# Delta rule: how the keys reach their tokens, and where their sums of squares come from

## The chip, the core and the metric

The kernel runs on one core of a Trainium2 chip. The metric is the device time of one execution in microseconds; of several runs the median is taken. The core has TensorE (PE, with its weight loads PEld), VectorE (DVE), ScalarE (ACT), GpSimd (POOL) and SyncE (SP), which here only issues DMAs.

## The reference

One decoder layer on 4 sequences of 512 tokens with 512 features, all in float32: a gated delta rule (16 heads of 128), then cross attention, then causal attention, then a mixture of experts. The change lies in the delta rule:

```python
q = causal_conv(x @ Wq.T)   # 4 taps along the tokens, then silu; k and v alike
g = exp(-exp(A_log) * softplus(a + dt_bias));  beta = sigmoid(b)
q, k = l2norm(q), l2norm(k)                       # by head, over 128 features
def step(S, (q_t, k_t, v_t, g_t, beta_t)):
    error = v_t - g_t * (S.T @ k_t)
    S = g_t * S + outer(k_t, beta_t * error)
    return S, S.T @ q_t
```

The kernel computes the recurrence in chunks of 128 tokens: inside a chunk through the inverse of a triangular matrix made of the products of all keys, from chunk to chunk through the state S. For that each key is needed in two layouts: features on the partitions (`kT`, for products) and tokens on the partitions (`ktok`, for the update of the state, scaled to `kdec`), and the sum of squares of each token's key (`ss`).

## The kernel before

The delta rule takes the first 1790 us or so. Its unit is a pair of heads of one sequence; 4 sequences x 8 pairs make 32 rounds (`NP`, line 1107). A round m is a set of generators that are advanced in turns (`turns`, line 192): for each step of `stage3(m)` two steps of `stage1(m + 2)`, one of `stage2_values(m + 1)`, two of the inversions for pair m + 1, one of `output(m - 1)`, and around a change of sequence some of `prologue`. A `yield` in a generator ends its step. So the place of a line among the `yield`s of its generator sets what it stands beside.

- `conv` (line 592) projects 128 features (TensorE, L598, into a PSUM tile `pb`), scales on ScalarE (L606), adds three shifted copies on VectorE (L609) and applies silu (L612).
- `stage1` (line 617): the two keys by `conv`; then, in one step for each head, four TensorE transposes into a PSUM tile (L641), a copy to `ktok` (L643) and four squares with sums (L646) on ScalarE; then `ss` is clamped (L652, VectorE) and raised to the power -1/2 on GpSimd (L653), with the small products `ee`, `ke`, `nr` (L654 to L657); two scans on VectorE make the decays `em` (L662) from a row loaded by DMA (`rows(0)`, L625); in the next two steps `em` is scaled by `ee` on ScalarE (L458), the products of the keys are made (L671, a PSUM tile `pb`), and `at` = -products x `em` on VectorE (L674) goes to DRAM (L675). `load_blocks` (L740) brings its diagonal blocks to the inversion. Then come the queries and, in `decayed`, `kdec` from `ktok` (L458).
- `stage2_inverse` (line 743) eliminates in 31 steps on GpSimd (L751, L752; in the first two rounds on VectorE).
- `stage2_values` (line 788): values by `conv`, then `brought`: VectorE transposes 32x32 blocks into the SBUF tile `vt`, which has one buffer (L798), four DMAs write it to DRAM (`v_d`, L801), one reads it back with tokens on the partitions (`vn`, L806), and it is scaled (L809).
- `stage3` (line 852) joins the inverse from its blocks, then goes through the four chunks: `pk` and `r` (L918, L921), `pu` and its ScalarE copy `u` (L928, L930), the state (L938, L943 or L941), the outputs (L946, L948).
- `output` (line 973) projects to the 512 features (L992) and adds up in `xa` (L997).

GpSimd, VectorE and ScalarE run in the order in which this code issues (`manual_schedule`, line 1089). The orders of TensorE and of SP's DMA queue are left to the framework's planner. [...] The DMAs that these steps name are issued by SP.

Of the kernel before, what the change touches and what calls it, by code (L numbers as in the profile page):

```python
# [31 lines left out]
F32 = mybir.dt.float32  # L32
BF16 = mybir.dt.bfloat16
AF = mybir.ActivationFunctionType
ALU = mybir.AluOpType
AX = mybir.AxisListType
# [3 lines left out]
P = 128  # L40
B, S, D = 4, 512, 512
NT = B * S // P
TB = S // P
# [3 lines left out]
HG = 2  # L47
# [57 lines left out]
def decoder(ctx: ExitStack, tc: tile.TileContext, a: dict, out: bass.AP):  # L105
    nc = tc.nc
# [6 lines left out]
    ident = tab[:, C_ID, :]  # L113
# [68 lines left out]
    def run(*gs):  # L182
        for g in gs:
            for _ in g:
                pass
# [17 lines left out]
    dram = ctx.enter_context(tc.tile_pool(name="dram", bufs=1, space=DRAM))  # L203
# [174 lines left out]
    with ExitStack() as st:  # L378
# [10 lines left out]
        def lasting(m, name, of, shape):  # L389

            own = m % of == (B * NHG - 1) % of
            return live[own].tile(shape, F32, name=name, bufs=HG * (1 if own else of - 1))
# [59 lines left out]
        def chunks(t):  # L452
            return t.rearrange("p c j -> p (c j)")

        def scale(dst, src, by, p):

            for c in range(TB):
                nc.scalar.activation(dst[:, c, :], src[:, c, :], AF.Identity, scale=by[:, p * TB + c : p * TB + c + 1])  # L458

        def behind(engine):  # L460

# [122 lines left out]
        def load_weights(m, *what, by=nc.sync):  # L584

            for n in what:
                if m < B * NHG:
                    t = (s1 if n < 2 else s2).tile([P, KD, HG * P], F32, name=f"w{n}", bufs=1)
                    by.dma_start(t, a["a_w"][m % NHG][:, n])
                    weights[m, n] = t  # L590
# [23 lines left out]

        keys, pairs = {}, {}

        def stage1(m):

            b, hg = divmod(m, NHG)
            hh = slice(hg * HG, (hg + 1) * HG)  # L620
            wk, wq = weights.pop((m, 1)), weights.pop((m, 0))

            def rows(n):
                t = s1.tile([P, HG, S], F32, name=f"row{n}", bufs=1)
                nc.sync.dma_start(chunks(t), g_d[b, n, hg * HG * TB : (hg + 1) * HG * TB].rearrange("c t -> (c t)").partition_broadcast(P))  # L625
                return [t[:, p, :] for p in range(HG)]

            kT, kt = [], []
            ss = small.tile([P, HG * TB], F32, name="ss", bufs=2)
            for p in range(HG):  # L630
                t = lasting(m, "kT", 3, [P, S])
                yield from conv(b, hg, p, 1, wk, t)
                kT.append(t)
                yield
            xnT, beta, gam, ngam, gend, gall = seqs[b]
            gb = rows(0)
            load_weights(m + 1, 1)
            for p in range(HG):
                tp = p_b.tile([P, TB, P], F32, name="pb")
                for c in range(TB):  # L640
                    nc.tensor.transpose(tp[:, c, :], kT[p][:, c * P : (c + 1) * P], ident)  # L641
                t = s1.tile([P, TB, P], F32, name="ktok")
                nc.scalar.copy(t, tp)  # L643
                kt.append(t)
                for c in range(TB):
                    nc.scalar.activation(tp[:, c, :], tp[:, c, :], AF.Square, accum_out=ss[:, p * TB + c : p * TB + c + 1])  # L646
                yield

            rk, ee, ke = (small.tile([P, HG * TB], F32, name=n, bufs=2) for n in ("rk", "ee", "ke"))
            nr = small.tile([P, HG * TB], F32, name="nr", bufs=4)  # L650
            flat = lambda t: t[:, hh, :].rearrange("p h c -> p (h c)")
            nc.vector.tensor_scalar(ss, ss, 1e-24, None, ALU.max)  # L652
            nc.gpsimd.tensor_tensor(rk, ss, mhalf[:, 0 : HG * TB], ALU.pow)  # L653
            nc.gpsimd.tensor_tensor(ee, rk, rk, ALU.mult)  # L654
            nc.gpsimd.tensor_tensor(ee, ee, flat(beta), ALU.mult)
            nc.gpsimd.tensor_tensor(ke, ee, flat(gend), ALU.mult)
            nc.gpsimd.tensor_tensor(nr, ss, rk, ALU.mult)  # L657
            em = []
            for p in range(HG):

                e = s1.tile([P, TB, P], F32, name="em")
                nc.vector.tensor_tensor_scan(chunks(e), gb[p], id4, 0.0, ALU.mult, ALU.add)  # L662
                em.append(e)
                yield
            ats = []
            for p in range(HG):
                scale(em[p], em[p], ee, p)
                pk = p_b.tile([P, TB, P], F32, name="pb")
                for c in range(TB):
                    k_ = kT[p][:, c * P : (c + 1) * P]  # L670
                    nc.tensor.matmul(pk[:, c, :], k_, k_, start=True, stop=True)  # L671
                at = lasting(m, "at", 2, [P, TB, P])
                ats.append(at)
                nc.vector.scalar_tensor_tensor(at, pk, -1.0, em[p], ALU.mult, ALU.mult)  # L674
                nc.sync.dma_start(squares(at_d[m % SLOTS][p * TB : (p + 1) * TB]), at)  # L675
                yield
            load_blocks(m, ats)
            mb = rows(1)

            qh, qg, pt, sq, kd_ = [], [], [], [], []  # L680

            def product(p):
                pq = p_b.tile([P, TB, P], F32, name="pb")
                for c in range(TB):
                    cs = slice(c * P, (c + 1) * P)
                    nc.tensor.matmul(pq[:, c, :], kT[p][:, cs], qh[p][:, cs], start=True, stop=True)
                t = lasting(m, "pt", 3, [P, TB, P])
                nc.vector.tensor_tensor(t, pq, em[p], ALU.mult)
                pt.append(t)

            def decayed(p):
                t = lasting(m, "kdec", 2, [P, TB, P])
                scale(t, kt[p], ke, p)
                kd_.append(t)

            for p in range(HG):
                q = s1.tile([P, S], F32, name="qh")
                c = conv(b, hg, p, 0, wq, q)
                yield from itertools.islice(c, 2)
                if p:  # L700
                    product(0)
                yield from c
                qh.append(q)
                g = lasting(m, "qg", 3, [P, S])
                nc.gpsimd.tensor_tensor(g, q, mb[p], ALU.mult)  # L705
                qg.append(g)
                t = w2.tile([P, S], F32, name="cv", bufs=5)
                nc.scalar.activation(t, q, AF.Square)
                sq.append(t)
                yield  # L710
            load_weights(m + 1, 0)
            decayed(0)
            yield

            pss = p_b.tile([P, HG, P], F32, name="pb")
            for p in range(HG):
                for c in range(TB):
                    nc.tensor.matmul(pss[c * 32 : (c + 1) * 32, p, :], tab_a[:, C_ONE, 0:32], sq[p][:, c * P : (c + 1) * P], start=True, stop=True)
            sr = small.tile([P, HG, P], F32, name="sr", bufs=1)
            nc.scalar.copy(sr, pss)  # L720

            rq = small.tile([P, HG * TB], F32, name="rq", bufs=2)
            for p in range(HG):
                nc.sync.dma_start(rq[p * P // HG : (p + 1) * P // HG, :], sr[:, p, :].rearrange("(c x) (n k) -> x c n k", x=32, k=HG * TB)[0])
            yield
            product(1)
            yield
            decayed(1)
            yield
            keys[m] = (kT, kd_, qg, pt, nr, rq)  # L730
# [57 lines left out]
        def stage2_values(m):  # L788
# [5 lines left out]

            def brought(p, t):

                x = w2.tile([P, 4, TB, 32], F32, name="vt", bufs=1)
                nc.vector.transpose(x.rearrange("p b k i -> p k b i"), t.rearrange("p (k b j) -> p k b j", b=4, j=32))  # L798
                d = dram.tile([P, 4, P], F32, name="v_d", bufs=4)
                for q in range(4):  # L800
                    nc.sync.dma_start(d[:, q, :].rearrange("(b j) x -> j b x", b=4), x[q * 32 : (q + 1) * 32].rearrange("p b k i -> p b (k i)"))  # L801
                yield
                yield
                v = w2.tile([P, 4, TB, 32], F32, name="vn", bufs=4)
                v_.append(v.rearrange("p a k i -> p k a i"))
                nc.sync.dma_start(v.rearrange("p a k i -> p a (k i)"), d)  # L806
                yield
                yield
                nc.vector.tensor_tensor(v, v, nr[:, p * TB : (p + 1) * TB].unsqueeze(1).unsqueeze(3).to_broadcast([P, 4, TB, 32]), ALU.mult)  # L809
# [1115 lines left out]
```

## Time and profile before

| | us |
|---|---|
| median of 3 runs | 3317.46 (3315.84 to 3320.69) |
| the profiled execution, whole time | 3312.34 |
| its span | 3310.5 |
| TensorE busy in the span | 3134.8 (95%) |
| VectorE / ScalarE / GpSimd busy | 1877.9 / 1603.0 / 1487.7 |
| L641, transposes of the keys: TensorE busy | 40.8 (x256) |
| L643 and L646, copies, squares and sums: ScalarE busy | 37.7 (x64), 67.1 (x256), 49.7 (x256) |
| L662, scans: VectorE busy | 74.7 (x64) |
| L671, products of the keys: TensorE busy | 66.9 (x512) |
| L798, block transposes of the values: VectorE busy | 45.4 (x64) |

In a line of the timeline stand the start in us from the start of the span, the time it lasted, the engine, the line of the code, the operation, output<-inputs by the program's names, the tile's size and how many instructions are merged; in brackets the idle time of the engine ahead of it and what ended it. In a line of the table by stretch stand the stretch, its length, the busy time of PE, PEld, DVE, ACT and POOL (with the number of instructions), the granted TensorE clock, the share of DMA time and GB/s. In a line of the waits stand the total wait in us, how often, and the longest. PEq and SPq are the engines' sequencers; SPq lines are issues of DMAs. Matmuls overlap, so that busy times of PE are more than its throughput; the distance of the weight loads (PEld) shows that.

### The profile page before, as it was taken

The page shows a single profiled execution, that of the slowest core. Times are in us where ns is not written, and L with a number is a line of the kernel's source. Part 1 is how long each engine was busy: PE and PEld are TensorE (multiplying, and loading weights), DVE is VectorE, ACT ScalarE, POOL GpSimd, SP SyncE. Part 2 cuts the span into 40 slices and gives each one's busy share as a digit, 9 for nine tenths or more (in the row PEclk, how much of TensorE's full clock was granted, in tenths as well). Part 3 has the DMA queues.
Part 4 walks back from the last instruction along what each step waited for, and adds up shares of the span by engine and source line. Part 5 has one row for each costly group of instructions (what it writes and reads, how often), then busy time and mean ns, then how long its engine had stood idle before and what let it go on. Part 6 is the DMA issues. An engine that isn't in the chain of part 4 may idle for free. (4 is left out here: it accounts for less than half of the span.)

```text
span 3310.5 us, 48238 instructions
## 1 busy us (share of the span) xinstructions
PE 3134.8 (95%) x15759; PEld 1754.4 (53%) x15759; DVE 1877.9 (57%) x4248; ACT 1603.0 (48%) x4391; POOL 1487.7 (45%) x2780
## 2 busy tenths in 40 slices
PE   5899999999999999999997789999999999999998
PEld 3455555555555555555554445555555555555444
DVE  5765565656655556555554566556665665646311
ACT  3445555455554455545453355555555555645222
POOL 1166757677666776666764211112211221121443
PEclk8999999999999999999998899999999999999999
DMA  6454545545455545564454455556645555567443
GB/s 172 126 160 132 156 126 148 166 139 159 127 151 153 162 133 141 146 175 134 140 137 133 153 181 180 177 159 185 186 165 166 186 169 155 173 198 260 102 90 61
DMA packets 537117, 509.68 MB, mean 154 GB/s; under 512 B 230453, under 2 KB 378443, under 8 KB 536737
## 3 DMA queue, kind: packets, MB, share of 16 engines
q1 hardware_dynamic: 523696, 478.17, 48.7%
q0 software_dynamic: 11728, 25.58, 3.7%
q8 instruction: 126, 2.06, 0.3%
q10 hardware_dynamic: 1440, 2.84, 0.3%
q14 instruction: 127, 1.03, 0.1%
HBM read 428.01 MB, written 78.47 MB: 153 GB/s over the span
## 5 line engine op out<-in xcount | busy, mean ns | idle before, releaser
L598 PE MATMUL pb<-xnT,w 128*128 128x512 f32 x2048 | 953.1, 602 | 3.4 <-DVE g_a L519 2.0
L598 PEld LDWEIGHTS pb<-xnT,w 128*128 128x128 f32 x2048 | 366.8, 192 | 355.4 <-issue 344.6
L609 DVE SCALAR_TENSOR_TENSOR cv<-pb,pp,cv 128x510 f32<-128x510 f32 (+2 forms) x576 | 424.5, 746 | 107.6 <-ACT cv L606 94.4
L752 POOL TENSOR_TENSOR iT<-iT,iW 64x126 f32<-64x126 f32 (+22 forms) x930 | 349.6, 376 | 72.9
L751 POOL TENSOR_TENSOR iW<-iA,iT 64x126 f32<-64x126 f32 (+22 forms) x930 | 327.3, 352 | 65.6
L1287 PE MATMUL pb<-c_q,hT 128*128 128x512 f32 x768 | 353.7, 601 | 2.4 <-ACT x_in L1359 1.3
L1206 POOL TENSOR_TENSOR rope_s<-q,tab 128x128 f32<-128x128 f32 x80 | 45.1, 563 | 479.7 <-DVE q L1317 367.1
L992 PE MATMUL pb<-wot,og 128*128 128x512 f32 x512 | 250.4, 612 | 5.9 <-DVE xa L997 4.5
L1287 PEld LDWEIGHTS pb<-c_q,hT 128*128 128x128 f32 x768 | 142.2, 192 | 156.6 <-issue 146.8
L606 ACT ACTIVATE cv<-pb,pp 128x512 f32<-128x512 f32 x192 | 148.5, 774 | 125.4 <-PE pb L598 120.2
L653 POOL TENSOR_TENSOR rk<-ss,mhalf 128x8 f32<-128x8 f32 x32 | 78.0, 2438 | 252.2 <-DVE ss L652 252.2
L306 ACT ACTIVATE x_e<-pb,nm,x_step 128x256 f32<-128x256 f32 x256 | 141.2, 565 | 59.5 <-DVE nm L302 56.1
L1353 PE MATMUL pb<-kT,qT 128*128 128x256 f32 (+3 forms) x576 | 163.2, 409 | 0.8 <-ACT og L1359 0.7
L1400 PE MATMUL pw<-wot,oT 128*128 128x512 f32 x344 | 162.5, 599 | 0.3 <-DVE oT L1392 0.3
L705 POOL TENSOR_TENSOR qg<-qh,row 128x512 f32<-128x512 f32 x64 | 91.7, 1432 | 143.1 <-ACT qh L612 131.8
L997 DVE TENSOR_TENSOR xa<-pb,xa 128x512 f32<-128x512 f32 x112 | 76.9, 688 | 137.2 <-PE pb L992 137.2
L992 PEld LDWEIGHTS pb<-wot,og 128*128 128x128 f32 x512 | 90.4, 192 | 89.6 <-issue 73.4
L612 ACT ACTIVATE qh<-cv 128x512 f32<-128x512 f32 x64 | 40.4, 631 | 200.2 <-DVE cv L609 200.2
L809 DVE TENSOR_TENSOR vn<-vn,nr 128x512 f32<-128x512 f32 x64 | 46.2, 721 | 156.4 <-DMA vn<-v_d 156.4
L1802 PE MATMUL pb<-w_gu,eT 128*128 x288 | 129.8, 593 | 3.1 <-issue 3.1
L1386 ACT COPY eT<-pb 128x512 f32<-128x512 f32 x160 | 91.5, 597 | 84.6 <-PE pb L1384 83.6
L132 POOL TENSOR_TENSOR rms_r<-rsq,mhalf 128x1 f32<-128x1 f32 x48 | 27.3, 570 | 222.2 <-DVE rsq L131 222.2
(435 smaller groups left out, 6265.8 us busy)
## 6 DMA issues: line engine op xcount, KB each, us to landing
c_q<-in_c_wq_dram SPq DMA_DIRECT2D x128, 512.0 KB
w<-in_a_w_dram SPq DMA_DIRECT2D x124, 512.0 KB
wot<-in_c_wo_dram SPq DMA_DIRECT2D x86, 512.0 KB
row<-g_d SPq DMA_DIRECT2D x64, 512.0 KB
c_o<-in_c_wo_dram SPq DMA_DIRECT2D x42, 512.0 KB
at_d<-at SPq DMA_DIRECT2D x64, 256.0 KB
rrow<-r_d SPq DMA_DIRECT2D x32, 512.0 KB
v_d<-vt SPq DMA_DIRECT2D x256, 64.0 KB
```

Of the source, the lines that this page charges most:

```text
L306: nc.scalar.activation(e[:, 2 * r + g, :], ps[r][:, g, :], AF.Exp, bias=nm[:, r, g : g + 1], scale=step[:, h : h + 1], accum_out=ssum[:, g ...
L598: nc.tensor.matmul(pj, wt[:, kd, p * P : (p + 1) * P], xnT[:, kd, :], start=kd == 0, stop=kd == KD - 1)
L606: nc.scalar.activation(ac, pj, AF.Identity, bias=cb[:, m, h : h + 1], scale=cw[:, m, h, 3:4])
L609: nc.vector.scalar_tensor_tensor(ac[:, j:], pj[:, : S - j], cw[:, m, h, 3 - j : 4 - j], ac[:, j:], ALU.mult, ALU.add)
L705: nc.gpsimd.tensor_tensor(g, q, mb[p], ALU.mult)
L751: eng.tensor_tensor(u, A[:, i, i + 1 :].unsqueeze(2).to_broadcast([nb, n, w]), T[:, i, :w].unsqueeze(1).to_broadcast([nb, n, w]), ALU.mult)
L752: eng.tensor_tensor(T[:, i + 1 :, :w], T[:, i + 1 :, :w], u, ALU.add)
L992: nc.tensor.matmul(pw, og[p][:, c * P : (c + 1) * P], wot[:, p, :], start=p == 0, stop=p == HG - 1)
L1287: nc.tensor.matmul(pj, hT[:, kd, :], w[:, kd % 2, :], start=kd == 0, stop=kd == KD - 1)
L1353: nc.tensor.matmul(ps[:, m, k * P : (k + w) * P], qT[g][:, n + m, :], kT[:, g, j : j + w, :], start=True, stop=True)
L1400: nc.tensor.matmul(pw, oT[:, h + m, :], w[:, m, :], start=g == 0 and h + m == 0, stop=g == 3 and h + m == 3)
L1802: nc.tensor.matmul(pg, hT[:, kd, :], w_gu[:, bass.ds(e, 1), kd, :, :], start=kd == 0, stop=kd == KD - 1)
```

## The change

The helper `turned_out` takes over from the values' `brought` what it did first: the block transposes into `vt` and the four writes to DRAM. `stage1` uses it for the keys too. Its own `brought` does a key's transposes and writes, lets two steps pass, and in the fourth step reads it back to `ktok`. Key 0's runs beside `conv` of key 1, key 1's beside the scans and products. `vt` still has one buffer, now for keys and values; `v_d` has 6 instead of 4.

The scans of `em` move ahead to where the transposes were. The products of the keys move one turn ahead of the scaling of `em`: two steps make both, and both PSUM tiles stay until `at` two steps later. In these steps VectorE multiplies the products by four identity matrices (`id4`) into `at` and sums each row, which gives the diagonal, so `ss`. TensorE's transposes and ScalarE's copies, squares and sums are gone. `scale` takes a source with one more dimension, since `ktok` now lies in blocks of 32 features.

```diff
+        def turned_out(t):
+            x = w2.tile([P, 4, TB, 32], F32, name="vt", bufs=1)
+            nc.vector.transpose(x.rearrange("p b k i -> p k b i"), t.rearrange("p (k b j) -> p k b j", b=4, j=32))
+            d = dram.tile([P, 4, P], F32, name="v_d", bufs=6)
+            for q in range(4):
+                nc.sync.dma_start(d[:, q, :].rearrange("(b j) x -> j b x", b=4), x[q * 32 : (q + 1) * 32].rearrange("p b k i -> p b (k i)"))
+            return d
...
+            def brought(t):
+                d = turned_out(t)
+                yield
+                yield
+                yield
+                k = s1.tile([P, 4, TB, 32], F32, name="ktok")
+                nc.sync.dma_start(k.rearrange("p a k i -> p a (k i)"), d)
+                kt.append(k.rearrange("p a k i -> p k a i"))
+            beside = []
             for p in range(HG):
                 t = lasting(m, "kT", 3, [P, S])
-                yield from conv(b, hg, p, 1, wk, t)
+                for _ in conv(b, hg, p, 1, wk, t):
+                    for g in beside:
+                        next(g, None)
+                    yield
                 kT.append(t)
                 yield
+                beside.append(brought(t))
             gb = rows(0)
             load_weights(m + 1, 1)
+            em, pks, ats = [], [], []
             for p in range(HG):
-                tp = p_b.tile([P, TB, P], F32, name="pb")
+                e = s1.tile([P, TB, P], F32, name="em")
+                nc.vector.tensor_tensor_scan(chunks(e), gb[p], id4, 0.0, ALU.mult, ALU.add)
+                em.append(e)
+                for g in beside:
+                    next(g, None)
+                yield
+            for p in range(HG):
+                pk = p_b.tile([P, TB, P], F32, name="pb")
                 for c in range(TB):
-                    nc.tensor.transpose(tp[:, c, :], kT[p][:, c * P : (c + 1) * P], ident)
-                t = s1.tile([P, TB, P], F32, name="ktok")
-                nc.scalar.copy(t, tp)
-                kt.append(t)
-                for c in range(TB):
-                    nc.scalar.activation(tp[:, c, :], tp[:, c, :], AF.Square, accum_out=ss[:, p * TB + c : p * TB + c + 1])
+                    k_ = kT[p][:, c * P : (c + 1) * P]
+                    nc.tensor.matmul(pk[:, c, :], k_, k_, start=True, stop=True)
+                pks.append(pk)
+                at = lasting(m, "at", 2, [P, TB, P])
+                ats.append(at)
+                nc.vector.tensor_tensor(chunks(at), chunks(pk), id4, ALU.mult)
+                nc.vector.tensor_reduce(ss[:, p * TB : (p + 1) * TB], at, AX.X, ALU.add)
+                for g in beside:
+                    next(g, None)
                 yield
...
             for p in range(HG):
                 scale(em[p], em[p], ee, p)
-                pk = p_b.tile([P, TB, P], F32, name="pb")
-                for c in range(TB):
-                    k_ = kT[p][:, c * P : (c + 1) * P]
-                    nc.tensor.matmul(pk[:, c, :], k_, k_, start=True, stop=True)
-                at = lasting(m, "at", 2, [P, TB, P])
-                ats.append(at)
-                nc.vector.scalar_tensor_tensor(at, pk, -1.0, em[p], ALU.mult, ALU.mult)
+                at = ats[p]
+                nc.vector.scalar_tensor_tensor(at, pks[p], -1.0, em[p], ALU.mult, ALU.mult)
                 nc.sync.dma_start(squares(at_d[m % SLOTS][p * TB : (p + 1) * TB]), at)
                 yield
+            run(*beside)
...
             def decayed(p):
                 t = lasting(m, "kdec", 2, [P, TB, P])
-                scale(t, kt[p], ke, p)
+                scale(t.rearrange("p c (a i) -> p c a i", i=32), kt[p], ke, p)
```

More of the change, by code (lines that the diff above doesn't have):

```diff
@@ L457, in scale @@
             for c in range(TB):
-                nc.scalar.activation(dst[:, c, :], src[:, c, :], AF.Identity, scale=by[:, p * TB + c : p * TB + c + 1])
+                nc.scalar.activation(dst[:, c], src[:, c], AF.Identity, scale=by[:, p * TB + c : p * TB + c + 1])
         def behind(engine):
@@ L657, in stage1 @@
             nc.gpsimd.tensor_tensor(nr, ss, rk, ALU.mult)
[L658 to L665, printed above, removed]
             for p in range(HG):
                 scale(em[p], em[p], ee, p)
-                pk = p_b.tile([P, TB, P], F32, name="pb")
-                for c in range(TB):
-                    k_ = kT[p][:, c * P : (c + 1) * P]
-                    nc.tensor.matmul(pk[:, c, :], k_, k_, start=True, stop=True)
-                at = lasting(m, "at", 2, [P, TB, P])
-                ats.append(at)
-                nc.vector.scalar_tensor_tensor(at, pk, -1.0, em[p], ALU.mult, ALU.mult)
+                at = ats[p]
+                nc.vector.scalar_tensor_tensor(at, pks[p], -1.0, em[p], ALU.mult, ALU.mult)
                 nc.sync.dma_start(squares(at_d[m % SLOTS][p * TB : (p + 1) * TB]), at)
                 yield
+            run(*beside)
             load_blocks(m, ats)
@@ L795, in brought @@
             def brought(p, t):
[L797 to L801, printed above, removed]
+                d = turned_out(t)
                 yield
```

## The prediction

> **What bounds the kernel now.** I read the header and the slices of the page first, then the busy time by stretch, then the waits of TensorE inside the delta rule (200 to 1650 us), then the timeline of one round, engine by engine. The round that starts near 895 us stands for the others: from 216 to 1714 us the copy of `u` (L930) ends 6.75 or 6.76 us after the key sums (L652) begin in each of 29 rounds.
>
> ```profile
> PE 3134.8 (95%) x15759; PEld 1754.4 (53%) x15759; DVE 1877.9 (57%) x4248; ACT 1603.0 (48%) x4391; POOL 1487.7 (45%) x2780
> 800.00:1000.00 200.00, 194.61 (x1127) 113.62 (x1126) 119.12 (x218) 106.48 (x294) 135.69 (x285) 0.99 0.54 151
> ```
>
> TensorE is busy 194.61 of 200 us there and every other engine has a third or more free. So TensorE's own work is the bound: a microsecond less of it is a microsecond gained, but only as long as its queue never runs dry. Now TensorE around the removed transposes, and where that stretch ends:
>
> ```profile
> 910.33 0.47 PEld L641 LDWEIGHTS pb<-tab,kT 128*128 128x128 f32 x4
> 911.12 0.42 PEld L641 LDWEIGHTS pb<-tab,kT 128*128 128x128 f32 x4 [0.32 <-ACT kT L612]
> 924.20 0.61 PE L938 MATMUL ps<-u,kdec 128*128 128x128 f32 x4
> ```
>
> Eight transposes hold TensorE 0.47 + 0.42 us, with 0.32 us of waiting for the second key. The third line is the state update of chunk 1: it is the first instruction that needs the chain below. That chain, on VectorE, GpSimd and ScalarE, which all run in the order in which the code issues:
>
> ```profile
> 910.91 0.68 DVE L997 TENSOR_TENSOR xa<-pb,xa 128x512 f32<-128x512 f32 x1
> 911.69 0.71 DVE L798 STREAM_TRANSPOSE vt<-cv 128x512 f32<-128x512 f32 x1
> 913.53 0.69 DVE L997 TENSOR_TENSOR xa<-pb,xa 128x512 f32<-128x512 f32 x1 [1.13 <-PE pb L992]
> 916.31 0.17 DVE L652 TENSOR_SCALAR ss<-ss 128x8 f32<-128x8 f32 x1 [2.09 <-ACT pb L646]
> 916.39 2.33 DVE L662 TENSOR_TENSOR_SCAN em<-row,tab_a 128x512 f32<-128x512 f32 x2
> 918.64 0.58 DVE L921 SCALAR_TENSOR_TENSOR r<-ps,ngam,vn 128x128 f32<-128x128 f32 x2
> 920.95 0.69 DVE L674 SCALAR_TENSOR_TENSOR at<-pb,em 128x512 f32<-128x512 f32 x1 [1.73 <-ACT em L458]
> ```
>
> ```profile
> 916.63 2.42 POOL L653 TENSOR_TENSOR rk<-ss,mhalf 128x8 f32<-128x8 f32 x1 [7.48 <-DVE ss L652]
> 919.41 0.20 POOL L655 TENSOR_TENSOR ee<-ee,beta 128x8 f32<-128x8 f32 x1
> 919.64 2.44 ACT L458 ACTIVATE em<-em,ee 128x128 f32<-128x128 f32 x8 [3.04 <-POOL ee L655]
> 922.00 0.76 ACT L606 ACTIVATE cv<-pb,pp 128x512 f32<-128x512 f32 x1
> 922.66 0.41 ACT L930 COPY u<-ps 128x128 f32<-128x128 f32 x2
> ```
>
> The reader should see a ladder: key sums (`ss`) at 916.31, the power on GpSimd, the scaling of `em` on ScalarE, `at`, and behind the scaling, in ScalarE's queue, the copy of `u` that ends at 923.07. TensorE needs `u` at 924.20. The ladder has 1.1 us to spare, no more.
>
> **The change, part by part.**
>
> *Removed.* Per round 8 transposes: 0.89 us of TensorE, and the 0.32 us wait, since the products now come a turn later: 1.21 us, over 32 rounds 39 us. On ScalarE per round two copies of 0.58 us and eight squares with their sums (about 0.40 us apart): 4.4 us. It is not the bound: no gain by itself.
>
> *Added to VectorE*, per round: two block transposes (0.71 us, L798), two products with the identity (0.69 us, as L688, PSUM times SBUF, 128x512) and two reductions. No reduction from SBUF of 4 groups is in the trace; L300 and L1356 take 0.68 and 0.69 us from PSUM for 512 elements, L1356 0.55 us for 384. I take 0.69, with 0.55 and 0.75 (L609) as ends, which moves the sum by 0.3 us. Together 4.2 us, on an engine with 40% free; what counts is where. The first key's transposition comes in the third turn, where VectorE waits for TensorE anyway (3.24 us before L997 at 907.42): free.
>
> *The order on VectorE.* By the code, between `xa` at 910.91 and `ss` it will run: scan, block transpose of key 1, scan, block transpose of value 0, `xa`, product, reduction, product, reduction, two `r`, `ss`. Key 1 and value 0 share **one** buffer `vt`. The second transpose can't write before the four DMAs of the first have landed. Their issue:
>
> ```profile
> 912.43 1.92 SPq L801 DMA_DIRECT2D v_d<-vt  x4
> ```
>
> By the landing records of the trace, the four of the first value of a round have landed 3.2 to 3.4 us after the transpose ended in most rounds, 4.4 in some; those of the second value 3.2 to 6.0. I take 3.35. So, from 911.59: scan 1.17 (half of 2.33) to 912.76; transpose to 913.47; scan to 914.64; `vt` free at 913.47 + 3.35 = 916.82, a new wait of 2.18 us with all of VectorE behind it; transpose to 917.53; `xa` to 918.22; 4 x 0.69 to 920.98; `r` to 921.56. `ss` begins at 921.56 instead of 916.31: **5.25 us late**, of which 2.18 are the wait on `vt`.
>
> *What hangs on it.* After `ss` the ladder is unchanged: the first `at` ends 5.33 us and `u` 6.76 us after `ss`, so at 926.9 and 928.3. TensorE reaches its state update 1.21 us earlier than before, at 923.0. Can it do other work meanwhile? Nearly all of its work needs one of the four PSUM slots `pb`, and already now it waits for one at this place (L671 behind ScalarE's squares):
>
> ```profile
> PEld pb L671 <- ACT pb L646: 5.0, 21, 0.2
> ```
>
> After the change the two key products hold a slot each from their matmuls until `at`, instead of being made just ahead of `at`; value 1's projection and query 0's hold the other two until VectorE has convolved them, which stands behind `at`. All four are taken at 923.0, so TensorE stands until the first `at` gives a slot back at 926.9 and query 1's projection can start (if the planner put it ahead), or until `u` at 928.4. The hole is 4.0 us, at most 5.4. Against 924.20 the round is longer by 927.0 - 924.2 = 2.8 us, at most 4.2. Later work doesn't give it back: TensorE is full for the rest of the round.
>
> *The hole and the clock.* The trace shows what such a hole does:
>
> ```profile
> 873.20:876.60 3.40, 1.50 (x11) 1.23 (x11) 3.26 (x9) 2.94 (x5) 2.02 (x4) 1.00 0.48 154
> 876.70:880.00 3.30, 3.30 (x8) 1.75 (x7) 3.12 (x9) 0.47 (x2) 2.68 (x8) 0.50 0.43 86
> ```
>
> Two gaps of 1.9 and 1.0 us in one stretch of 3.4 us, and the granted clock is 0.50 in the next, which costs half of it, 1.7 us. A 4.0 us hole covers 2.9 us of such a stretch in (4.0 + 3.4 - 5.8)/3.4 = 0.47 of its positions: 0.8 us a round, 1.5 for the long hole. [...]
>
> *Behind other work, at nothing.* GpSimd gets `ss` 5.25 us later, but the two inversion steps of that turn (1.7 us) now go ahead of the power; its inverse ends 3.6 us later, at 936.2 instead of 932.6, and its blocks are wanted at 942.84 in a round that is itself later. Without that cover, up to 3 us a round. SP gets 10 more issues a round, 4.3 us; the key blocks are read back some six turns before `decayed` needs them. DMA traffic grows by 64 x 0.5 MB = 34 of 510 MB, with the DMA engines half free; if it stretches the landing to 4.4 us, 1 us a round. The strided read in `scale` is taken at its 0.39 us; ScalarE is idle 3.90 us soon after.
>
> *The start.* In the first round `ss` comes at 42.44, but its scans wait for `row` until 44.72. After: 44.72 + 2.33 + 0.71 + 2.76 puts `ss` at 50.5 and the first `at`, with that round's power of 1.65 us, at about 55 instead of 48.1. VectorE then waits for that very inverse (6.70 us before L751 at 55.95): 7 us, between 0 and 14.
>
> *Sum.* 30 rounds with a stage 1 beside a stage 3: 30 x (2.8 + 0.8) = 108, plus 7: 115 us. The profiled execution took 3312.3 us (span 3310.5): 3427. The median of the runs is 5 us higher, so I say 3430. Ends of this case: without clock loss and with a short start 30 x 2.8 = 84, or 3400, less 20 if the reductions are cheap or a projection fits earlier; 30 x 5.7 = 171, or 3490 with the later `u`.
>
> [...]
>
> **Rivals.**
> 1. *TensorE never runs dry* (faster). Place: TensorE's queue between 923.0 and 927.0; price: none. It needs 4 us of work that holds no `pb` slot, or key products ordered so late that the slots stay free. For it: TensorE's and SP's order is not written by hand, and waits are below 3% now. Against it: only 1.1 us of slack is in the ladder, and four slots. Then 39 us are gained and some of the 7 lost: 3280. It decides if `ss` moves by less than 1.1 us.
> 2. *The wait on `vt` is short or absent, the rest holds.* `ss` is 3.1 us late, the hole 1.8 us and too short for the clock: 0.6 to 2.0 us a round, 20 to 60 plus 7: 3345 to 3385.
> 3. *Gains and losses cancel*, hole about 1.2 us: 3317.
>
> **Chances.** Forecast 0.53, rival 2 0.20, rival 3 0.05, rival 1 0.22. Slower by over 0.2% (about what a measurement here can tell) 0.73, within 0.05, faster 0.22. The range takes all of the forecast's ends and rivals 2 and 3, and a little of rival 1: 3285 to 3490. The forecast's own is 3380 to 3490.
>
> **What would show it.** Right: VectorE waits about 2 us ahead of the value transposes, released by `v_d`; `ss` 9 to 10 us after the third `xa` (now 4.7); ScalarE idle some 9 us ahead of `em`; TensorE with one gap of 4 us a round and stretches at half clock; rounds of 55 us instead of 52. Wrong: `ss` less than 6 us after that `xa`, or TensorE filled through the wait.

## The result and the profile after

The changed kernel takes 3529.7 us (median of 5 runs, 3524.68 to 3530.15) against 3318.53 us (5 runs), a ratio of 1.0626 with a 95% interval of 1.0614 to 1.0639: 211 us slower. The prediction said 3430, 3285 to 3490. The sign and the place were right, the size was not.

The profiled execution of after took 3530.15 us, its span is 3528.3 us. First the page's header line, then the stretch shown of before, the long stretch of after, and the same long stretch of before (columns: stretch, length, busy time of PE, PEld, DVE, ACT, POOL with counts, granted clock, DMA share, GB/s).

```profile
PE 3185.3 (90%) x15503; PEld 1765.5 (50%) x15503; DVE 1990.3 (56%) x4440; ACT 1482.1 (42%) x3815; POOL 1467.7 (42%) x2780
```

```profile
800.00:1000.00 200.00, 181.38 (x1036) 105.36 (x1035) 124.02 (x230) 87.83 (x215) 122.81 (x265) 0.97 0.53 145
```

```profile
300.00:1700.00 1400.00, 1251.14 (x6885) 713.88 (x6885) 809.59 (x1401) 562.15 (x1417) 839.70 (x1779) 0.96 0.54 150
```

```profile
300.00:1700.00 1400.00, 1370.27 (x8003) 795.12 (x8002) 810.54 (x1394) 730.21 (x2064) 964.10 (x2006) 1.00 0.52 147
```

TensorE was busy for 98% of this stretch and is now busy for 89%. No other engine has taken its place: VectorE is as busy as it was, ScalarE and GpSimd less. When every engine has more idle time, the time went into waiting. It went there evenly. From the first `ss` to the last, 31 rounds, each round is 6.3 us longer: 25.3 us in the first four, 171.0 in the other 27. The first `ss` comes 12.8 us later (55.2 instead of 42.4). 12.8 + 196.3 = 209 of the 218 us by which the two profiled spans differ (the medians differ by 211); the other 9 us come behind the last `ss`.

One round of after, VectorE first (the brackets hold the idle time ahead of the instruction and what ended it):

```profile
1316.80 0.68 DVE L1019 TENSOR_TENSOR xa<-pb,xa 128x512 f32<-128x512 f32 x1
1317.40 1.21 DVE L667 TENSOR_TENSOR_SCAN em<-row,tab_a 128x512 f32<-128x512 f32 x1
1318.53 0.69 DVE L620 STREAM_TRANSPOSE vt<-kT 128x512 f32<-128x512 f32 x1
1319.14 1.18 DVE L667 TENSOR_TENSOR_SCAN em<-row,tab_a 128x512 f32<-128x512 f32 x1
1325.45 0.71 DVE L620 STREAM_TRANSPOSE vt<-cv 128x512 f32<-128x512 f32 x1 [5.13 <-DMA v_d<-vt]
...
1329.80 0.16 DVE L690 TENSOR_SCALAR ss<-ss 128x8 f32<-128x8 f32 x1
1333.59 0.69 DVE L699 SCALAR_TENSOR_TENSOR at<-pb,em 128x512 f32<-128x512 f32 x1 [3.62 <-ACT em L458]
```

This is the order that the prediction wrote down, with the new wait where it put it; but the wait is 5.13 us here, not 2.18, and `ss` starts 12.3 us after the third `xa` ends (median of the rounds 12.2; before 4.7; forecast 10.0). What lies behind it on ScalarE and on TensorE's weight loads:

```profile
1332.28 2.45 ACT L458 ACTIVATE em<-em,ee 128x128 f32<-128x128 f32 x8 [13.32 <-POOL ee L693]
```

```profile
1323.75 0.19 PEld L598 LDWEIGHTS pb<-xnT,w 128*128 128x128 f32 x1 [0.24 <-issue]
1326.79 0.45 PEld L598 LDWEIGHTS pb<-xnT,w 128*128 128x128 f32 x2 [2.85 <-DVE xa L1019]
```

ScalarE stands 13.32 us ahead of the scaling. TensorE runs dry already **while VectorE waits on `vt`**: the `xa` behind that wait would free a PSUM slot. It runs dry again on the ladder. Over 300 to 1700 us its waits are (total us, times, longest):

```profile
PEld pb L598 <- DVE xa L1019: 53.9, 18, 4.1
PEld ps L960 <- ACT u L952: 46.8, 57, 5.3
PEld pb L598 <- DVE at L699: 40.1, 15, 3.7
PEld pb L712 <- ACT qh L612: 24.7, 22, 1.9
```

Not one hole of 4 us per round, but several. The clock follows them:

```profile
1323.50:1326.90 3.40, 1.38 (x4) 0.31 (x4) 1.45 (x3) 0.00 (x0) 0.00 (x0) 1.00 0.54 189
1326.95:1330.30 3.35, 3.35 (x4) 1.30 (x5) 2.94 (x7) 0.00 (x0) 0.26 (x1) 0.50 0.72 185
```

From 150 to 1800 us the clock stands at half for 133 us, against 24 before; over the same 31 rounds, from the first `ss` to the last, for 169 us against 31.

The wait comes from the landing of key 1's four writes. They have landed 6.0 us after its transpose ended (median of the rounds away from a change of sequence; 3.32 to 6.78), not 3.35. SP's queue at this moment, and the DMA share behind it (second fence, last but one column):

```profile
1318.56 0.38 SPq L1001 DMA_DIRECT2D wot<-in_a_wo_dram  x1
1319.24 1.78 SPq L623 DMA_DIRECT2D v_d<-vt  x4
```

```profile
1320.15:1323.50 3.35, 3.35 (x17) 2.15 (x16) 0.17 (x1) 0.00 (x0) 0.00 (x0) 1.00 0.98 297
```

A load of 512 KB, the output weights `wot`, is issued 0.7 us ahead of the key's writes, and the DMA engines are 98% busy.

### The profile page after: what moved, and what is told of

Read it like the earlier page. It is cut to its first block, busy times and chain, and to the rows that moved or that the text cites. A ratio compares the mean times of both kernels' runs of the same rounds, so it can differ in the third digit from the quotient of the medians.

```text
span 3528.3 us, 48001 instructions
## 1 busy us (share of the span) xinstructions
PE 3185.3 (90%) x15503; PEld 1765.5 (50%) x15503; DVE 1990.3 (56%) x4440; ACT 1482.1 (42%) x3815; POOL 1467.7 (42%) x2780
## 3 DMA queue, kind: packets, MB, share of 16 engines
q10 hardware_dynamic: 1440, 2.84, 0.3%
## 5 line engine op out<-in xcount | busy, mean ns | idle before, releaser
L598 PE MATMUL pb<-xnT,w 128*128 128x512 f32 x2048 | 1007.6, 625 | 117.4 <-DVE at L699 62.2
L598 PEld LDWEIGHTS pb<-xnT,w 128*128 128x128 f32 x2048 | 372.1, 198 | 475.8 <-issue 330.3
L778 POOL TENSOR_TENSOR iT<-iT,iW 64x126 f32<-64x126 f32 (+22 forms) x930 | 353.9, 381 | 72.9
L458 ACT ACTIVATE em<-em,ee 128x128 f32<-128x128 f32 x256 | 78.2, 388 | 390.2 <-POOL ee L693 390.2
L691 POOL TENSOR_TENSOR rk<-ss,mhalf 128x8 f32<-128x8 f32 x32 | 52.6, 1642 | 387.8 <-DVE ss L690 387.8
```

What stands on the lines that cost most here:

```text
L598: nc.tensor.matmul(pj, wt[:, kd, p * P : (p + 1) * P], xnT[:, kd, :], start=kd == 0, stop=kd == KD - 1)
L778: eng.tensor_tensor(T[:, i + 1 :, :w], T[:, i + 1 :, :w], u, ALU.add)
```

## The experiments

**Theory A** (the prediction's): what counts is how late `ss` comes, through the wait on `vt` and VectorE's added work; the first 2.45 us of lateness are free (5.25 us late gave 2.8 a round). **Theory B**: it is something else, the traffic, the PSUM slots, SP's queue, or VectorE's order as a whole. Lateness below is the median, over the rounds away from a change of sequence, of the time from the end of the third `xa` to `ss`, less 4.72; a round is the mean of the last 27. A result without a range is a single execution; the kernel before took 3315 to 3320 us on the same chips.

### Two buffers for `vt`

```diff
-            x = w2.tile([P, 4, TB, 32], F32, name="vt", bufs=1)
+            x = w2.tile([P, 4, TB, 32], F32, name="vt", bufs=2)
```

> The changed kernel with two buffers `vt` instead of one, nothing else. Theory (the wait on `vt` and the order on VectorE make the key sums late, and TensorE runs dry behind them): the wait ahead of the value's block transpose, 3.8 to 5.4 us a round in the changed kernel, goes; `ss` begins about 8 us after the third `xa` instead of 12.4; of the 211 us that the change cost some 110 to 160 come back: 3370 to 3420. Rival (the added DMA traffic and the ten more issues a round on SP's queue cost the time by themselves): about 3530, as the traffic is the same.

Measured: 3397.41 us (before 3317.22), as expected; rounds of 55.70 us, `ss` 2.4 us late. The wait is gone:

```profile
1232.54 0.68 DVE L1019 TENSOR_TENSOR xa<-pb,xa 128x512 f32<-128x512 f32 x1
...
1234.27 0.69 DVE L620 STREAM_TRANSPOSE vt<-kT 128x512 f32<-128x512 f32 x1
...
1235.98 0.68 DVE L620 STREAM_TRANSPOSE vt<-cv 128x512 f32<-128x512 f32 x1
...
1240.31 0.16 DVE L690 TENSOR_SCALAR ss<-ss 128x8 f32<-128x8 f32 x1
```

Between the two transposes stands only the scan. So 132 of the 211 us hang on the one buffer. But 80 remain, and 2.14 us a round, where the free 2.45 us would have left none. TensorE's longest waits in this kernel (300 to 1700 us: total us, times, longest) are not for a PSUM slot, but for `u`, the copy behind the scaling on ScalarE, and for `r` on VectorE:

```profile
PEld ps L960 <- ACT u L952: 72.9, 50, 3.4
PEld ps L950 <- DVE r L943: 38.4, 47, 1.5
```

That is 2.9 and 1.5 us a round. Before, `u` kept TensorE waiting for 0.7 us in the whole execution, and `r` for 0.5 us a round.

### The sums alone, and the route alone

The first keeps TensorE's transposes and the copy to `ktok`, and takes the sums from the diagonal in the new order. The second is the kernel before with the keys' route through `vt` and DRAM; transposes and squares stay for the sums, only the copy to `ktok` goes.

```diff
+                tp = p_b.tile([P, TB, P], F32, name="pb")
+                for c in range(TB):
+                    nc.tensor.transpose(tp[:, c, :], kT[p][:, c * P : (c + 1) * P], ident)
+                t = s1.tile([P, TB, P], F32, name="ktok")
+                nc.scalar.copy(t, tp)
```

> One half of the change alone: scans first, products early, sums of squares from the diagonal; but the keys get to their tokens by TensorE transposes and a ScalarE copy as before, with no block transposes and no DRAM for keys. Theory: no wait on `vt`, but 2.3 us of scans and 2.8 us of products and sums stand ahead of `ss`, so it comes about 7.8 us after the third `xa` instead of 4.7; TensorE keeps its 0.9 us of transposes; 1 to 3 us a round and a slower start: 3350 to 3420. Rival (DMA): 3318, as there is no added traffic.

```diff
+                beside.append(brought(t))
...
-                nc.scalar.copy(t, tp)
                 for c in range(TB):
                     nc.scalar.activation(tp[:, c, :], tp[:, c, :], AF.Square, accum_out=...)
+                for g in beside:
+                    next(g, None)
```

> The other half alone: the kernel before, with its transposes and ScalarE squares kept for the sums, but `ktok` by VectorE's block transposes and DRAM, with the one shared `vt`. Theory: key 1 and value 0 meet at `vt` as in the change, VectorE waits some 4 to 6 us there, `xa` and `ss` come 3 to 5 us late: 1 to 4 us a round, 3350 to 3440. Rival (DMA): most of the 211 us, 3480 or more.

Measured: 3368.47 (`ss` 2.4 us late, +1.29 a round) and 3366.70 (some 1.8 us late, +1.27), both as expected. Each half costs some 50 us; together they cost 211. In the route alone VectorE waits on the shared buffer too:

```profile
DVE vt L620 <- DMA v_d<-vt: 92.6, 28, 4.9
```

That is 3.6 us for each of 25.5 rounds, yet `ss` is only some 1.8 us late: there VectorE waited 2.09 us for ScalarE's squares before, and the new wait takes the place of that one.

### The traffic alone

The kernel before with the keys' writes, taken from `kT` itself, and a read into a tile that nothing uses.

```diff
                 kT.append(t)
+                for q in range(4):
+                    nc.sync.dma_start(d[:, q, :].rearrange(...), t[q * 32 : (q + 1) * 32].rearrange(...))
+                nc.sync.dma_start(k, d)
                 yield
```

> The kernel before, and beside it the added DMAs alone: per key four writes of 64 KB to DRAM, straight from `kT`, and one read back of 256 KB into a tile that nothing uses; no VectorE work, no wait of an engine on them. Theory: no more than 10 us over the kernel before, 3318 to 3330. Rival (DMA): 3400 or more.

Measured: 3330.01 (3326.58 to 3332.81, 5 runs), ratio 1.0036 (1.0018 to 1.0054): 13 us, the upper end of what was expected. `ss` is not late at all (4.72), but VectorE's wait for the values that are read back (`vn`) grows from 126.2 to 143.7 us between 300 and 1700 us. 34 MB of traffic and ten issues a round are no free edit, but a small one.

### The keys' writes on ScalarE's queue

```diff
-                d = turned_out(t)
+                d = turned_out(t, nc.scalar)
```

> The changed kernel, with the four writes of each key's blocks issued by ScalarE's queue instead of SP's; still one `vt`. Theory: what made the wait on `vt` longer than the 2.18 us of my prediction is SP's queue, in which a 512 KB weight load is issued just ahead of key 1's writes (landing 3.5 to 6.5 us after the transpose instead of 3.35). On another queue they land nearer to 3.4 us, the wait falls from some 4.9 to 2 to 3 us, and 40 to 100 us come back: 3430 to 3490. Rival (the landing is slow because all DMAs share the engines behind the queues): no shorter, 3510 to 3540.

Measured: 3534.85 (before 3320.06), and key 1's blocks land after 6.17 us, where the change has 6.0; VectorE's waits on `vt` are 118.9 us between 300 and 1700 us (the change 110.7). My expectation failed and its rival's range, 3510 to 3540, held: the delay is not in SP's queue. Key 0's landing fell from 9.40 to 3.22 us, since its writes no longer stand in SP's queue behind the DMA `r_d<-rq` (in the change's round shown above that DMA is issued at 1314.34 and the writes at 1314.71, 6.05 us after key 0's transpose has ended). Little waits for those: in the changed kernel key 1's transpose does in 6 rounds, 4.3 us in all.

### The output weights out of the way

The change, with `wot` loaded behind `load_blocks`, from round 3 on.

```diff
-            wot = ao.tile([P, HG, D], F32, name="wot", bufs=2)
-            nc.sync.dma_start(wot, a["a_wo"][hg])
+            wot = wots.pop(m, None) or load_wot(m)
...
             load_blocks(m, ats)
+            if m > 4:
+                with behind(mybir.EngineType.SP):
+                    wots[m - 2] = load_wot(m - 2)
```

> The changed kernel, one `vt`, but from round 3 on the 512 KB load of the output weights `wot` is issued behind that round's `load_blocks` instead of when its slot comes free, which in the changed kernel is 0.6 us ahead of the end of key 1's block transpose. Theory (key 1's blocks land late because that load fills the DMA engines just ahead of them): they land in about 3.7 us as in the runs where `wot` came later, not in 6.0, the wait on `vt` falls by about 2.3 us a round, and with the hole and the half clock that go with it 60 to 110 us come back: 3420 to 3470. Rival (the landing is slow for another reason, such as the added key traffic itself): 3515 to 3540.

Measured: the landing falls to 3.89 us, so the load in flight was what delayed it.

```profile
DVE vt L626 <- DMA v_d<-vt: 75.8, 29, 4.5
```

This is 3.2 us a round of 58.9, where the change has 110.7 us in 23.4 rounds, 4.7 each. But the time is 3502.19 (before 3315.1): 187 us over before instead of 211, so some 25 us came back, not 60 to 110. `ss` is still 6.0 us late, near the forecast's 5.25, and a round is 5.3 us longer, not 3.6. So the landing is not all that was mis-sized.

### The sums ahead of the scans, with one and with two buffers

The two scans move from ahead of the products to behind `ss`, where VectorE waits for GpSimd and ScalarE anyway.

```diff
-            for p in range(HG):
-                e = s1.tile([P, TB, P], F32, name="em")
-                nc.vector.tensor_tensor_scan(chunks(e), gb[p], id4, 0.0, ALU.mult, ALU.add)
-                ...
             for p in range(HG):
                 pk = p_b.tile([P, TB, P], F32, name="pb")
...
             nc.gpsimd.tensor_tensor(nr, ss, rk, ALU.mult)
+            for p in range(HG):
+                e = s1.tile([P, TB, P], F32, name="em")
+                nc.vector.tensor_tensor_scan(chunks(e), gb[p], id4, 0.0, ALU.mult, ALU.add)
+                ...
```

> The changed kernel with the products and their sums ahead of the scans on VectorE (the scans go between the power and the scaling, as before the change); still one `vt`. Theory: `ss` comes 2.3 us of scans and 0.6 us of `r` earlier, but the wait on `vt` stays and grows by what stood beside it, so about 8 us after the third `xa`: 3370 to 3420. Rival (what costs is that the products hold two PSUM slots, whatever the order; they are now held longer): 3530 or more.

> Both: products and sums ahead of the scans, and two buffers `vt`. Theory: `ss` about 4.9 us after the third `xa` (4.7 in the kernel before), so TensorE does not run dry, and 0.9 us of transposes and 0.3 us of waiting are saved each round against 12 us that the added traffic costs in all: 3285 to 3320, as fast as the kernel before or a little faster. Rival (PSUM slots held longer): 3360 or more.

Measured: with one buffer 3388.49 (`ss` 2.5 us late, rounds +2.1). With two, 3306.06 (3301.59 to 3308.63, 5 runs) against 3320.06, ratio 0.9959 (0.9945 to 0.9973): **faster than both kernels**, by 0.4% against the kernel before, which is small but clear of the noise. In the median `ss` is 0.34 us earlier than before, 4.38 us after the third `xa`. In the round shown it is 5.35, since a normalization stands in the same place:

```profile
1219.21 0.68 DVE L1019 TENSOR_TENSOR xa<-pb,xa 128x512 f32<-128x512 f32 x1
...
1221.13 0.70 DVE L620 STREAM_TRANSPOSE vt<-kT 128x512 f32<-128x512 f32 x1
...
1223.04 0.70 DVE L620 STREAM_TRANSPOSE vt<-cv 128x512 f32<-128x512 f32 x1
...
1225.24 0.16 DVE L681 TENSOR_SCALAR ss<-ss 128x8 f32<-128x8 f32 x1
1225.31 2.33 DVE L690 TENSOR_TENSOR_SCAN em<-row,tab_a 128x512 f32<-128x512 f32 x2
...
1229.87 0.69 DVE L699 SCALAR_TENSOR_TENSOR at<-pb,em 128x512 f32<-128x512 f32 x1 [1.73 <-ACT em L458]
```

```profile
300.00:1700.00 1400.00, 1369.68 (x7922) 782.42 (x7921) 913.17 (x1574) 636.63 (x1609) 972.95 (x2029) 1.00 0.60 169
```

VectorE now does its scans inside the ladder and waits 1.73 us for `em`, as before, instead of 3.62; TensorE is as full as before, and a round is 0.88 us shorter. The same work, in another order and with a second buffer, gains where the change lost.

### PSUM slots

The products are copied into `at` by ScalarE, so that their slots come free. On top of the fastest kernel and on top of the one with two buffers.

```diff
                 nc.vector.tensor_reduce(ss[:, p * TB : (p + 1) * TB], at, AX.X, ALU.add)
+                nc.scalar.copy(at, pk)
+                pks[p] = at
```

> The same, and ScalarE copies each product from PSUM into `at` after its sum is taken, so that the slot is free some 3 to 6 us earlier; VectorE's last multiplication then works in SBUF. Theory (slots are not what bounds once `ss` is early): within 15 us of the run with both. Rival (PSUM slots): 30 to 60 us less than it.

> The changed kernel with two `vt` (3397) and, besides, ScalarE copies each product from PSUM into `at` after its sum, so that the two slots do not wait for the power and the scaling. Theory (the state update waits for `u` behind the late scaling on ScalarE, whatever the slots): 3375 to 3400, a part of the hole filled by query 1's projection at most. Rival (the held slots are what makes TensorE run dry): 3340 or less.

Measured: 3302.87 (3298.82 to 3306.31, 4 runs; ratio 0.9949, 0.9932 to 0.9965), not told apart from 3306.06; and 3402.89 beside 3397.41, just above the expected range. Slots that are free do not help where `ss` is 2.4 us late: rounds of 55.72 against 55.70, and TensorE waits as long for `u` (75.6 against 72.9 us). The prediction had the slots as what keeps TensorE from filling the hole; with two buffers that is not so. In the change itself, whose longest waits above are for slots (53.9 and 40.1 us, for `u` 46.8), it was not tried.

### How much is a late ladder, and VectorE's work behind it?

Both start from the kernel before. One computes the power twice; the other adds two instructions on VectorE behind each `at`.

```diff
             nc.gpsimd.tensor_tensor(rk, ss, mhalf[:, 0 : HG * TB], ALU.pow)
+            nc.gpsimd.tensor_tensor(rk, ss, mhalf[:, 0 : HG * TB], ALU.pow)
```

> The kernel before with the power of the key sums on GpSimd computed twice (the same values): the ladder is late by one power, some 2.4 us, while VectorE's queue and TensorE's work are as before. By the prediction's step (1.1 us to spare in the ladder ahead of TensorE's state update, the rest of the delay a hole in TensorE's work) the round grows by 1.3 us and the time by 31 x 1.3 = 40: 3350 to 3365. Rival, from the runs so far (about 0.85 us a round for each us that the key sums come late, from the first one, since no slack is left anywhere in the round): 2.4 x 0.85 x 31 = 63: 3372 to 3395.

```diff
                 nc.sync.dma_start(squares(at_d[m % SLOTS][p * TB : (p + 1) * TB]), at)
+                for _ in range(2):
+                    nc.vector.tensor_tensor(em[p], em[p], em[p], ALU.max)
```

> The kernel before with two extra VectorE instructions behind each of the two products at, a maximum of em with itself, 128x512 (the values stay): some 2.6 us more in VectorE's order a round, behind the ladder instead of ahead of it. By the prediction's view (VectorE has 40% free and only what stands ahead of the key sums counts) it costs no more than a few us: 3318 to 3330. Rival (the whole in-order round of VectorE, where convolutions, state updates and transposes stand behind each other, is as tight behind the ladder as in it): 0.85 x 2.6 x 31 = 68: 3375 to 3395.

Measured, the first: 3351.65 (3346.08 to 3357.22, 2 runs; ratio 1.0103, 1.0054 to 1.0153), +0.98 us a round. The second power takes 1.64 us, so `at` is 1.71 us late and not 2.4: with 1.1 us to spare that would be 0.6 a round, by 0.85 for each microsecond 1.45. Neither; 0.57 for each microsecond. That the time lies in the first range, 3350 to 3365, is luck: the delay was smaller than expected and each microsecond of it dearer.

The second: 3378.06 (3376.62 to 3379.51, 2 runs; ratio 1.0183, 1.0151 to 1.0215), +1.85 us a round, as the rival said. The work added (group by line, between 300 and 1700 us: busy us, mean ns | idle us ahead) and TensorE's new wait:

```profile
L677 DVE TENSOR_TENSOR em<-em 128x512 f32<-128x512 f32 x100 | 71.0, 710 | 3.4
```

```profile
PEld ps L920 <- DVE state L945: 31.9, 22, 2.2
```

2.84 us a round of plain work on an engine that is 57% busy, and 65% of it ends up in the time; `ss` is not late here (4.72). My view that only work ahead of the sums counts is refuted. VectorE's order is tight behind the ladder too, since the state updates that TensorE waits for stand in it.

## Why the prediction was right and wrong

**Right: the mechanism and its direction.** The transposes of keys and values block each other in the one `vt`, and all of VectorE waits behind them; `ss`, the ladder and TensorE follow. The run with two buffers shows the first link (132 us of 211), the run with the sums first and two buffers the rest: with `ss` on time, the same parts are faster than before. The sums first with one buffer alone bring back 141 us, so the two shares overlap. Rival 1 (never dry) holds for that kernel, whose `ss` is not late, with 14 us of its 39, and not for the change. Rival 2 (no wait on `vt`) is the run with two buffers: 3397 us, above its 3345 to 3385.

**Right: the durations.** Product 0.68 us (forecast 0.69), reduction 0.69 (0.69), transpose 0.70 (0.71), strided scale 0.39 (0.39). The start cost 12.8 us, inside the 0 to 14, above the 7. The first key's transpose was free (VectorE waits for TensorE behind it still, 3.23 us ahead of the `xa` at 1313.32).

**Wrong, the term that failed first: "I take 3.35"**, the landing of key 1's blocks. It was read from the values' writes, in an order in which no large load stood ahead of them. After, key 1's writes stand right behind the 512 KB of `wot`, and land after 6.0 us. The wait is 4.7 us a round instead of 2.18, `ss` 7.5 us late instead of 5.25. The prediction did not ask what would be in flight ahead of the keys' writes; by the runs the delay goes with that load (3.89 us with it moved) and not with the queue (6.17 us on ScalarE's).

**Wrong, the second, and by the runs the larger: "5.25 late, longer by 2.8".** It lets the first 2.45 us of lateness go free, since `at` ended that much ahead of TensorE's state update in the old round (921.64 to 924.20, less 0.1), and, behind one hole, takes the rest of the round as full of TensorE's work. Fed with each kernel's measured lateness, that step, with its clock term (1.7 us times the share of positions, at most 1), gives:

| kernel | `ss` late, us | the step, us a round | measured |
|---|---|---|---|
| two `vt` | 2.4 | -0.1 | +2.14 |
| sums first, one `vt` | 2.5 | +0.1 | +2.1 |
| weights behind | 6.0 | 4.8 | +5.3 |
| the change | 7.5 | 6.8 | +6.3 |

The step is near where `ss` is very late, and fails where it is little late. What it had wrong there is what TensorE waits for. The prediction let the hole end when the first `at` frees a slot, for which the ladder had 2.45 us to spare, and kept `u`, for which it had 1.1, for the upper end. With two buffers TensorE waits 2.9 us a round for `u`, and free slots change nothing. `u` alone is no full account either: in this kernel it ends 5.9 us after `ss` instead of 6.75, so 2.4 us of lateness leave 2.4 - 0.85 - 1.1, some 0.4 of the 2.14 us. The wait for `r` is 1.0 us a round longer. The run with work behind `at`, where `ss` is on time and 65% of the added work ends up in the time, shows that VectorE's order has little room elsewhere too; that the change's own 4.2 us of work cost time in this way is likely, not shown.

**Wrong, the third: the clock term, 0.8 us a round.** It asked for 2.9 us of idleness in a stretch of 3.4, the sum of two gaps of the weight loads. TensorE itself was busy for 1.50 of the 3.40 us of that row (873.20:876.60), so it was idle for 1.9. With 1.9 the same formula, (4.0 + 3.4 - 3.8)/3.4, is over 1, and a 4.0 us hole costs the full 1.7 us: as an estimate 0.9 us a round more, 28 us in all. Measured over the 31 rounds are 138 us more at half clock, where four matmuls of L598 take 3.68 us (from 1326.79), against 1.88 at full clock (from 1309.68); so it cost at most half of that, 2.2 us a round. That a hole counts by its share of positions was my estimate; no run shows it.

**How much each.** A line through the first and last row of the table (2.14 at 2.38, 6.33 at 7.51) has 0.82 us for each microsecond late, and 4.5 at the forecast's 5.25. As an estimate from it: 1.85 us a round from the landing, 57 us in 31 rounds; 0.9 from the rest of the step, its clock term included, 28 us; one round more at 3.6; 5.8 from the start. The sum, 94 of the missing 96 us, is no test: the line goes through the change's own row. The test is the run with the weights moved, and it gives the landing less, some 25 us: with `ss` near the forecast's lateness it still costs 187 us, where the forecast had 115. Its `ss` moved by 1.5 of the 2.3 us, and its rounds by 1.0 us; what the load costs at its new place no run separates.

**"Costed at nothing."** The traffic's bound was 1 us a round, if it stretched the landing; alone it costs 13 us in all, and lengthens VectorE's wait for `vn` by 17.5 us between 300 and 1700 us, 0.5 us each time. GpSimd's later inverse was not priced by a run. That the parts cost more together (50 + 50 against 211) is read from the traces, not shown by a run of its own: in the route alone VectorE's wait lies partly in its old 2.09 us wait for the squares, in the sums alone there is no wait on `vt` at all; only together do both stand ahead of `ss`.

**Signs.** Wait released by `v_d`: seen, twice as long. `ss` 9 to 10 us after `xa`: 12.2. ScalarE idle 9 us: 12 to 13. One 4 us gap: several. Rounds 55 us: 59.9, where before's mean is 53.55.

**Open.** How much of the 211 us is the clock. At half clock for 138 us more from the first `ss` to the last, it can be at most 69; in the prediction it was 24. No run holds the holes fixed and the clock full. Which of VectorE's instructions behind `at` carries the 0.65 was not tried either.

## What to carry to other kernels

Work taken off the bounding engine paid here only where the engine that got it had room at that place in its order: VectorE's share of busy time, 57% before, did not tell, the wait displaced did. Put what the long chain needs first, and work that only fills (here the scans) into the chain's waits (with two buffers 3306.06 us instead of 3397.41); give a buffer that two streams share, with a DMA as reader, one copy for each (3397.41 instead of 3529.7). Take the landing time of a small transfer from a moment with the same large load in flight (here 6.0 us, not 3.35).

## What the runs showed of the hardware

The same power of 128x8 on GpSimd, on the same data, took 2.49 us beside VectorE's two scans and 1.64 us right after them (the kernel with two powers):

```profile
1252.66 2.49 POOL L653 TENSOR_TENSOR rk<-ss,mhalf 128x8 f32<-128x8 f32 x1 [2.02 <-DVE ss L652]
1255.22 1.64 POOL L654 TENSOR_TENSOR rk<-ss,mhalf 128x8 f32<-128x8 f32 x1
```

In the changed kernel, whose scans are over by then, it is 1.64 us too, and with the sums ahead of the scans 2.48 again (medians). So the changed kernel's ladder from `ss` to the end of `at` is 4.5 us, 0.8 shorter than the prediction took it, and the kernel is slower all the same.

The landing of four 64 KB writes went from 3.3 to 6.0 us with 512 KB issued 0.7 us ahead on the same queue, and to 6.17 from another queue.

The clock went to half after a stretch of 3.40 us with TensorE busy 1.38 us, so after 2.0 us of idleness, and stood there for 3.41 us, from 1326.88 to 1330.29. In the kernel before it did so after the stretch 873.20:876.60 with 1.50 us busy, 1.9 us of idleness, and stood there for 3.41 us too, from 876.66 to 880.07.
